# Storing layer 1's rows in rank order and gathering them by rank at the turn to layer 3, in a four-layer graph network

## The chip, the cores and the metric

The kernel runs on one core of one Trainium2 chip. The metric is the device time of one launch in microseconds (us), the median over runs. The core has TensorE (PE; its weight loads are listed apart as PEld), VectorE (DVE), ScalarE (ACT), GpSimd (POOL) and SyncE (SP). Each engine works through its own instructions in order; they wait for each other by semaphores. DMAs are issued here from SyncE, from ScalarE and, where rows are picked by an index (gather and scatter), from GpSimd; an instruction that waits holds up everything behind it in its engine's queue, DMAs included.

## The reference

Four layers over 2708 nodes with 128 features and an adjacency matrix of 2708 x 2708, of which about 0.6% is not zero. Each layer adds its result to its input and normalises over the features:

```python
x = _layernorm(x + _L0_gnn_ref(x, adj))       # (adj.T @ x) / column sums of adj
x = _layernorm(x + _L1_gnn_ref(x, adj, ...))  # messages: gelu(s_i + d_j + b), summed over j with adj_ij, an update MLP
x = _layernorm(x + _L2_gnn_ref(x, adj, ...))  # batch-normed adj @ (x @ W), leaky relu with 0.2
x = _layernorm(x + _L3_gnn_ref(x, adj, ...))  # GATv2 attention, 4 heads, weighted by adj
```

What matters here: x after layer 1 (in the kernel x2) is needed twice. Layer 2 multiplies it by W and by the adjacency matrix; and layer 2's residual adds it once more, row by row, to the batch-normed result.

## The kernel before

Nodes are tiled by 128 into 22 blocks (`BLOCKS`; the last has 20 nodes). Layer 0 is dense. In layers 1 and 3 the kernel uses lists of each node's neighbours, which it finds from the adjacency rows (`extract`, `lists`, `place`), and it sorts the nodes by how many neighbours they have: `rank[n]` is the place of node n in that order, and `perm` is the reverse, the node that stands at a place. Layer 1 works on blocks in rank order, layer 2's result and the batch norm on blocks in node order.

*Layer 1, the loop over 22 blocks* (`for i, b in enumerate(TURNS)`). `own_row` loads a block's rows `x_s` by SyncE (L868, three buffers). `messages` gathers neighbours' rows, one GpSimd gather of 128 rows for each place in the lists (L249, called at L905 through `gather_spaced`, which puts a clear of 200 bytes, L263, between two gathers of a table) into `msg` (five buffers of up to 8 gathers); VectorE adds (L907), ScalarE applies gelu (L910), VectorE weighs and sums (L893, L895). `spread` (L629 to L648) prepares layer 3's lists beside it. `update` runs TensorE (L921, L930 to L932), ScalarE (`agg_t` L928, gelu L937) and VectorE (L938 to L946), ends in `x_n`, the block's rows of x2 (L332 through `normalised`), sends them away (L947, the line that the change edits) and multiplies them by W of layer 2 (L948 to L953) into `xw`.

*Beside it*: `transposed` brings blocks of the adjacency matrix through TensorE transposes (L980), ScalarE copies (`at_sb`, three buffers, L985) and SyncE stores (L987) to `at_dram`, which holds the transposed matrix. The adjacency rows come by SyncE (L417) into the tiles of `ring`, nine slots of 128 x 2708 floats. From turn 11 on `layer2(k)` gathers rows of `at_dram` by `perm` into the same ring (`at_rows`, L1016) and accumulates in six PSUM banks (L1029; the column sums are put in by L1025).

*The turn to layer 3* (L1107 to L1246). When the banks are complete, VectorE and ScalarE compute the batch norm's mean and scale (L1132 to L1156) in `hb`; `masks(g)` makes seven sets of masks for layer 3 from index patterns that GpSimd writes (`jrow` L1158, `row_of` L1166, `start` L1168). Then, four blocks at a time, hb is scaled (L1196 to L1198), the residual x2 is added (L1201), the rows are normalised, scattered in rank order by GpSimd (`x3_dram`, L1215, through the helper at L266) and multiplied into layer 3's table `t2_dram`. Layer 3's own gathers (`g4`) start when that table is written.

*What sets the order.* Between L848 and L1246 a scheduler orders each engine's instructions by the program's order and its own estimate of when each is ready; in parts of layer 0 and in layer 3 the order is written out by hand. Tiles of a closed pool give up their place in memory to pools that are opened later, and these wait for the last use. The ring is opened as the first pool of layer 1 and closed with it.

The rows of x2 go through memory: the scatter at L947 puts the row at place p of block b into row `perm[p, b]` of `x2_dram`, so the table is in node order, and two loads of SyncE (L1114, L1115) bring it back whole.

Of the kernel before, what the change touches and what calls it, by code (L numbers as in the profile page):

```python
# [9 lines left out]
FP = mybir.dt.float32  # L10
# [5 lines left out]
P = 128  # L16
N = 2708
D = 128
NFULL = N // P
NREM = N - NFULL * P  # L20
NBLK = NFULL + 1
# [38 lines left out]
RING = 9  # L60
LW = 2 * SLOTS + 2
BLOCKS = [(b * P, min(P, N - b * P)) for b in range(NBLK)]
# [23 lines left out]
def gnn_resnorm_kernel(  # L86
# [21 lines left out]
    nc = tc.nc  # L108
# [135 lines left out]
    def natural(dram, b0, b1):  # L244

        return dram[b0 * P : b1 * P, :].rearrange("(b p) w -> p b w", p=P)
# [18 lines left out]
    def scatter(table, index, rows):  # L265
        return nc.gpsimd.indirect_dma_start(  # L266
            out=table,
            out_offset=bass.IndirectOffsetOnAxis(ap=index, axis=0),
            in_=rows,
            in_offset=None,  # L270
        ).ins
# [69 lines left out]

    graph = ExitStack()
    own_ps = graph.enter_context(tc.tile_pool(name="own_ps", bufs=1, space=PSUM))

    def banks(name):
        return [bank.tile([P, 512], FP, name=f"{name}{i}", tag="bank") for i in range(6)]

    with ExitStack() as layer:
        ring = layer.enter_context(tc.tile_pool(name="ring", bufs=RING))
        work = layer.enter_context(tc.tile_pool(name="work", bufs=1))  # L350
        small = layer.enter_context(tc.tile_pool(name="small", bufs=2))
        engine = mybir.EngineType
# [312 lines left out]
        for g in KINDS:  # L665
            j = 32 // g
# [250 lines left out]
        def update(b, x_s, x_st, parts):  # L917
            n = BLOCKS[b][1]
            tp = tail_ps.tile([P, 512], FP, name="tail")
            for i in range(2):  # L920
                nc.tensor.matmul(  # L921
                    tp[:, 0:n], lhsT=parts[0:n, i, :], rhs=ident[0:n, 0:n],
                    start=(i == 0), stop=(i == 1),
                )
            x_b = mine.tile([P, D], FP, name="x_b")
            nc.vector.tensor_tensor(x_b[0:n], x_s[0:n, 1, :], lnb[0:n], ALU.add)
            agg_t = mine.tile([P, P], FP, name="agg_t")
            nc.scalar.copy(agg_t[:, 0:n], tp[:, 0:n])  # L928
            pn = tp[0:n, P : 2 * P]
            nc.tensor.matmul(pn, lhsT=x_st[:, 0:n], rhs=u1_t, start=True, stop=False)  # L930
            nc.tensor.matmul(pn, lhsT=ones[0:1, 0:n], rhs=updb[0:1, :], start=False, stop=False)
            nc.tensor.matmul(pn, lhsT=agg_t[:, 0:n], rhs=u2_t, start=False, stop=True)  # L932
            new = mine.tile([P, 1, D], FP, name="new")
            x_n = mine.tile([P, 1, D], FP, name="x_n")
            sums = mine.tile([P, 2], FP, name="sums1")
            h, s0, s1 = new[0:n, 0, :], sums[0:n, 0:1], sums[0:n, 1:2]
            nc.scalar.activation(h, pn, AF.Gelu)  # L937
            nc.vector.scalar_tensor_tensor(  # L938
                h, h, 1.0, x_s[0:n, 1, :], ALU.mult, ALU.add, accum_out=s0
            )  # L940
            rstd = deviation(mine, n, 1, new[0:n], s0)
            nc.vector.scalar_tensor_tensor(h, h, s0, lnw[0:n], ALU.add, ALU.mult)
            nc.vector.scalar_tensor_tensor(
                h, h, rstd[0:n, 0:1], x_b[0:n], ALU.mult, ALU.add, accum_out=s1
            )
            normalised(mine, n, 1, new[0:n], s1, x_n[0:n])  # L946
            scatter(x2_dram, perm[0:n, b : b + 1], x_n[0:n, 0, :])  # L947
            nc.tensor.transpose(tp[:, 256 : 256 + n], x_n[0:n, 0, :], ident[0:n, 0:n])  # L948
            x_nt = mine.tile([P, P], FP, name="x_nt")
            nc.scalar.copy(x_nt[:, 0:n], tp[:, 256 : 256 + n])  # L950
            px = tp[0:n, 384:512]
            nc.tensor.matmul(px, lhsT=x_nt[:, 0:n], rhs=w2_l2, start=True, stop=True)
            nc.scalar.copy(xw[0:n, b, :], px)  # L953
# [58 lines left out]
        def layer2(k):  # L1012

            b, n = TURNS[k], BLOCKS[TURNS[k]][1]
            at = ring.tile([P, N], FP, name="at_rows", tag="rows")
            gather(at[0:n, :], at_dram, perm[0:n, b : b + 1])  # L1016
            weighed = small.tile([P, P], FP, name="weighed", bufs=1)
            nc.scalar.activation(
                weighed[0:n], ones[0:n], AF.Copy, scale=column_sum[0:n, b : b + 1]
            )  # L1020
            for ib in range(NBLK) if k == 0 else ORDER:
                i0, m = BLOCKS[ib]
                if ib == 21:

                    nc.tensor.matmul(  # L1025
                        accs2[5][:, 2 * D : 3 * D], lhsT=weighed[0:n], rhs=xw[0:n, b, :],
                        start=False, stop=False,
                    )
                nc.tensor.matmul(  # L1029
                    accs2[ib // 4][0:m, (ib % 4) * D : (ib % 4 + 1) * D],  # L1030
                    lhsT=at[0:n, i0 : i0 + m],
                    rhs=xw[0:n, b, :],
                    start=(k == 0 and ib % 4 == 0),
                    stop=(k == NBLK - 1 and ib in (3, 7, 11, 15, 19, 20)),
                )
# [10 lines left out]
        for i, b in enumerate(TURNS):  # L1046
# [34 lines left out]
            if i >= 11:  # L1081
                for k in range(2 * (i - 11), min(i, 2 * (i - 10))):
                    layer2(k)
        layer2(NBLK - 1)

# [21 lines left out]
    with ExitStack() as layer:  # L1109
        work = layer.enter_context(tc.tile_pool(name="bn", bufs=1))  # L1110
        small = layer.enter_context(tc.tile_pool(name="bn_small", bufs=2))
        hb = work.tile([P, NBLK, D], FP, name="hb")
        x2 = work.tile([P, NBLK, D], FP, name="x2")
        nc.sync.dma_start(x2[:, 0:NFULL, :], natural(x2_dram, 0, NFULL))  # L1114
        nc.sync.dma_start(x2[0:NREM, NFULL, :], x2_dram[NFULL * P : N, :])  # L1115
        a_all = keep.tile([P, HEADS, D], FP, name="a_all")
        nc.scalar.dma_start(a_all, att.partition_broadcast(P))
        w1_sb = keep.tile([P, HEADS, D], FP, name="w1_s")
# [75 lines left out]
        for b0, count, n in quads():  # L1194
            h = hb[0:n, b0 : b0 + count]
            nc.vector.tensor_tensor(h, h, broad(scale, n, count), ALU.mult)  # L1196
            nc.vector.tensor_tensor(h, h, broad(beta_row, n, count), ALU.add)
            nc.vector.scalar_tensor_tensor(h, h, 0.2, h, ALU.mult, ALU.max)  # L1198
            sums = small.tile([P, 4], FP, name="sums2")
            for j in range(count):  # L1200
                nc.vector.scalar_tensor_tensor(  # L1201
                    hb[0:n, b0 + j, :], hb[0:n, b0 + j, :], 1.0, x2[0:n, b0 + j, :],
                    ALU.mult, ALU.add, accum_out=sums[0:n, j : j + 1],
                )
            normalised(
                small, n, count, h, sums[0:n, 0:count], xs[0:n, b0 : b0 + count, :],
                newton=False,
            )
            w = (count - 1) * P + n
            nc.sync.dma_start(  # L1210
                t2_dram[b0 * P : b0 * P + w, HD : HD + D].rearrange("(b p) w -> p b w", p=n),
                xs[0:n, b0 : b0 + count, :],
            )
            for b in range(b0, b0 + count):
                did = scatter(x3_dram, rank[0:n, b : b + 1], xs[0:n, b, :])  # L1215
                for before in sent:
                    tc.declare_no_dep(
                        did, before, query=mybir.DependencyQuery.ANY_SYNC,
                        reason="each row has a place of its own",
                    )  # L1220
                sent.append(did)
            pt = bank.tile([P, 512], FP, name="pt_x3", tag="bank")
            for j in range(count):
                nc.tensor.transpose(
                    pt[:, j * P : j * P + n], xs[0:n, b0 + j, :], ident[0:n, 0:n]
                )
            xt = small.tile([P, 512], FP, name="xt3")
            nc.scalar.copy(xt[:, 0:w], pt[:, 0:w])
            for j in range(count):
                at = slice(j * P, j * P + n)  # L1230
                pm = bank.tile([P, 512], FP, name="pm_t", tag="bank")
                nc.tensor.matmul(pm[0:n], lhsT=xt[:, at], rhs=w2_sb, start=True, stop=True)
                pa = bank.tile([P, 512], FP, name="pa_t", tag="bank")
                nc.tensor.matmul(
                    pa[0:n, 0:HEADS], lhsT=xt[:, at], rhs=w_a2, start=True, stop=True
                )
                row = small.tile([P, HD], FP, name="t_row", bufs=4)
                nc.scalar.copy(row[0:n], pm[0:n])
                beta_t = small.tile([P, HEADS], FP, name="beta_t", bufs=4)
                nc.vector.tensor_copy(beta_t[0:n], pa[0:n, 0:HEADS])  # L1240
                r0 = (b0 + j) * P
                nc.sync.dma_start(t2_dram[r0 : r0 + n, 0:HD], row[0:n, :])
                nc.sync.dma_start(t2_dram[r0 : r0 + n, HD + D : RW], beta_t[0:n, :])
# [865 lines left out]
```

## Time and profile before

| what | value |
|---|---|
| median of three runs (lowest to highest) | 1891.95 us (1882.17 to 1901.53) |
| the profiled execution, time and span | 1903.62 and 1901.9 us |
| mean granted TensorE clock | 0.719 |
| busy: PE, PEld, DVE, ACT, POOL | 1279.9, 876.6, 1118.4, 822.5, 1094.0 us |
| GpSimd gathers in layer 1 / layer 2 / layer 3 | 368 / 22 / 400 |
| last x_n of layer 1 ends | 1011.1 us |
| layer 2's banks complete | 1020.8 us |
| first row block added at L1201 | 1043.5 us |
| first gather of layer 3's table | 1100.6 us |

All times that follow from the profile belong to one profiled execution, which took 11.7 us more than the median of the runs. A row of the groups reads: line, engine, operation, what it writes <- what it reads, how often, then busy time in us and mean ns of one, then the engine's idle time before it and what ended that. Digits in names are left out, so `x_dram` stands for `x2_dram` and `x3_dram`; what is read tells them apart. A matmul of 32-bit floats leaves two records. The starts of TensorE's records tell when an instruction was taken up, their ends are modelled; that TensorE was late shows in those who wait for it. "remote" as the end of a wait is a semaphore's change that the profile can't put to a recorded instruction.

### The profile page before, as it was taken

How to read it: one execution, taken by the hardware profiler on the slowest of the kernel's cores; microseconds unless marked ns; L12 is line 12 of the kernel's file. 1: busy time of each engine (PE TensorE's matmuls, PEld its weight loads, DVE VectorE, ACT ScalarE, POOL GpSimd, SP SyncE). 2: the span in 40 equal slices, each digit the busy share in tenths (PEclk: the TensorE clock that was granted, in tenths of full speed). 3: DMA queues.
4: the chain of work that ended last, by engine and by line, in shares of the span. 5: the costliest groups of instructions: out<-in, count | busy, mean ns of one | idle time of the engine just before them, and what ended most of it. 6: DMA issues, size and time to landing. Idle time of an engine off the chain costs nothing. (4 is left out here: it accounts for less than half of the span.)

```text
span 1901.9 us, 24866 instructions
## 1 busy us (share of the span) xinstructions
PE 1279.9 (67%) x5971; PEld 876.6 (46%) x5971; DVE 1118.4 (59%) x4643; ACT 822.5 (43%) x3508; POOL 1094.0 (58%) x1771
## 2 busy tenths in 40 slices
PE   7973413453456536556674758998889899788884
PEld 6973302342345435545563324454445455444543
DVE  8997546675534452333446526666667668565663
ACT  3565436443323211111111525565566567455662
POOL 1004777646766375764640476875776777766640
PEclk9986555555555666667766866788788989778785
DMA  8632557566545523324231574865565665745540
GB/s 286 245 138 87 135 130 208 170 172 180 142 119 143 173 66 117 113 95 143 83 104 45 165 226 136 221 199 162 166 201 172 184 185 167 220 139 174 162 115 7
DMA packets 167684, 289.71 MB, mean 152 GB/s; under 512 B 49600, under 2 KB 121502, under 8 KB 160429
## 3 DMA queue, kind: packets, MB, share of 16 engines
q0 software_dynamic: 60496, 190.77, 34.2%
q1 hardware_dynamic: 99489, 92.57, 15.7%
q10 hardware_dynamic: 7544, 4.69, 1.0%
q8 instruction: 50, 0.82, 0.2%
q14 instruction: 105, 0.86, 0.1%
HBM read 242.51 MB, written 45.36 MB: 151 GB/s over the span
## 5 line engine op out<-in xcount | busy, mean ns | idle before, releaser
L249 POOL DMA_INDIRECT g<-t_dram,idx x400 | 403.5, 1009 | 196.2 <-issue 124.8
L249 POOL DMA_INDIRECT msg<-d_dram,idx x368 | 350.3, 952 | 153.9 <-issue 114.5
L1401 ACT ACTIVATE sum_junk<-g 126x128 bf16<-126x128 f32 (+3 forms) x1200 | 352.6, 296 | 39.2 <-ACT sum_junk L1401 21.6
L1375 PE MATMUL z<-g,ident 126*126 126x512 f32 (+3 forms) x400 | 250.0, 757 | 0.6 <-issue 0.6
L1369 PE MATMUL z<-x,copies 32*126 32x512 f32 (+3 forms) x800 | 213.0, 769 | 39.5 <-issue 23.1
L1401 ACT ACTIVATION_READ_ACCUMULATOR sum_junk<-g 126x1 f32 (+3 forms) x1200 | 225.6, 188 | 0.0
L980 PE MATMUL pt_a<-ident,rows 128*128 128x128 f32 (+2 forms) x475 | 118.1, 409 | 136.8 <-issue 68.9
L263 POOL MEMSET pause<- 1x200 int8 x768 | 195.7, 255 | 1.5 <-remote 1.3
L1029 PE MATMUL acc<-x_nat,at_rows 128*128 128x128 f32 (+2 forms) x968 | 169.1, 337 | 32.7 <-issue 21.9
L1029 PEld LDWEIGHTS acc<-x_nat,at_rows 128*128 128x128 f32 (+2 forms) x968 | 152.5, 243 | 49.9 <-issue 35.8
L980 PEld LDWEIGHTS pt_a<-ident,rows 128*128 128x128 f32 (+2 forms) x475 | 86.8, 212 | 159.6 <-issue 78.9
L1375 PEld LDWEIGHTS z<-g,ident 126*126 126x126 f32 (+3 forms) x400 | 83.0, 231 | 166.4 <-issue 155.0
L1447 PE MATMUL po_s<-wm,g 126*128 126x24 f32 (+6 forms) x800 | 117.9, 301 | 53.8 <-DVE wm L1434 38.2
L431 PE MATMUL acc<-x_nat,rows 128*128 128x129 f32 (+3 forms) x1012 | 128.6, 288 | 26.6 <-DMA rows<-in_adj_dram 16.0
L1447 PEld LDWEIGHTS po_s<-wm,g 126*128 126x128 f32 (+3 forms) x800 | 115.1, 227 | 66.2 <-DVE wm L1434 42.1
L895 DVE SCALAR_TENSOR_TENSOR own<-msg,ls,own 128x128 f32<-128x128 f32 (+1 forms) x302 | 106.0, 351 | 66.6 <-ACT msg L910 23.9
L1567 DVE TENSOR_TENSOR g<-g,z 126x1024 f32<-126x1024 f32 (+3 forms) x100 | 121.6, 1216 | 39.4 <-PE z L1369 16.9
L431 PEld LDWEIGHTS acc<-x_nat,rows 128*128 128x128 f32 (+2 forms) x1012 | 122.8, 197 | 32.0 <-DMA rows<-in_adj_dram 17.0
L1393 DVE SCALAR_TENSOR_TENSOR g<-g,a_ps 126x1024 f32<-126x1024 f32 (+3 forms) x100 | 121.1, 1211 | 0.0
L1369 PEld LDWEIGHTS z<-x,copies 32*126 32x126 f32 (+3 forms) x800 | 63.9, 211 | 90.4 <-issue 56.4
L1385 DVE SCALAR_TENSOR_TENSOR g<-z,a 126x128 f32<-126x128 f32 (+3 forms) x400 | 91.6, 285 | 20.4 <-PE z L1375 9.4
L1568 DVE SCALAR_TENSOR_TENSOR g<-z,a 126x512 f32<-126x512 f32 (+3 forms) x100 | 68.6, 686 | 58.8 <-remote 23.2
(302 smaller groups left out, 2164.4 us busy)
## 6 DMA issues: line engine op xcount, KB each, us to landing
rows<-in_adj_dram SPq DMA_DIRECT2D x34, 1354.0 KB
at_dram<-at_sb SPq DMA_DIRECT2D x105, 256.0 KB
g<-t_dram,idx POOLq DMA_INDIRECT x400
msg<-d_dram,idx POOLq DMA_INDIRECT x368
t_dram<-t_row SPq DMA_DIRECT2D x21, 256.0 KB
x_s<-dx_dram SPq DMA_DIRECT2D x21, 128.0 KB
at_dram<-at_sb SPq DMA_DIRECT2D x21, 64.0 KB
t_dram<-x_nat SPq DMA_DIRECT2D x5, 256.0 KB
```

Source lines behind the costliest of these rows:

```text
L249: return nc.gpsimd.indirect_dma_start(out=dst, out_offset=None, in_=table[0:N, :], in_offset=bass.IndirectOffsetOnAxis(ap=index, axis=0),)
L263: paused[table.name] = nc.gpsimd.memset(pause, 0).ins
L431: nc.tensor.matmul(accs0[k][0:m, c0 : c0 + f1 - f0], lhsT=rows[0:n, j0 : j0 + m], rhs=x_nat[0:n, b, f0:f1], start=k not in started, stop=( ...
L895: nc.vector.scalar_tensor_tensor(to, m, v, last, ALU.mult, ALU.add)
L980: nc.tensor.transpose(pt[0:m, j, 0:n], rows[0:n, c0 : c0 + m], ident[0:n, 0:n])
L1029: nc.tensor.matmul(accs2[ib // 4][0:m, (ib % 4) * D : (ib % 4 + 1) * D], lhsT=at[0:n, i0 : i0 + m], rhs=xw[0:n, b, :], start=(k == 0 and i ...
L1369: nc.tensor.matmul(z2[0:e, r, :] if r < 2 else zs[r - 2][0:e], lhsT=copies[g][rows, j, :], rhs=own[b][1][rows, :], start=True, stop=r < 2, ...
L1375: nc.tensor.matmul(zs[r - 2][0:e], lhsT=ident[0:e, 0:e], rhs=g4[0:e, r, 0:HD], start=False, stop=True, skip_group_check=True,)
L1393: nc.vector.scalar_tensor_tensor(z, z, 0.0, a_ps[0:e].unsqueeze(1).to_broadcast((e, 2, HD)), ALU.max, ALU.mult)
L1401: nc.scalar.activation(junk[0:e], g4[0:e, r, hd * D : (hd + 1) * D], AF.Identity, accum_out=sc[0:e, r, hd : hd + 1],)
L1447: nc.tensor.matmul(po[:, p0 * HEADS : (p0 + g) * HEADS], lhsT=g4s[i][0:e, r, HD : HD + D], rhs=wm[0:e, 4 * i + r, :, :], start=True, stop= ...
L1567: nc.vector.tensor_tensor(z, z, z2[0:e], ALU.add)
```

## The change

Three things. The row blocks of layer 1 are stored as they are, in rank order, by a plain store that SyncE issues, in place of GpSimd's scatter. After the last `layer2` 22 gathers of GpSimd, one a block, fetch x2 by `rank`, so that each block arrives in node order; they go into two tiles that take slots of the ring (21 blocks in the one, the last block in the other), and L1201 reads them there. The two loads and the tile x2 of the batch-norm pool go. For this the ring is opened outside of layer 1, on the other side of the memory, and is kept until the batch norm is done. The gathers of layers 1 and 3 keep the clears between them, as before.

```diff
     own_ps = graph.enter_context(tc.tile_pool(name="own_ps", bufs=1, space=PSUM))
+    ring = graph.enter_context(tc.tile_pool(name="ring", bufs=RING, side="right"))
...
     with ExitStack() as layer:
-        ring = layer.enter_context(tc.tile_pool(name="ring", bufs=RING))
...
             normalised(mine, n, 1, new[0:n], s1, x_n[0:n])
-            scatter(x2_dram, perm[0:n, b : b + 1], x_n[0:n, 0, :])
+            nc.sync.dma_start(x2_dram[b * P : b * P + n, :], x_n[0:n, 0, :])
...
         layer2(NBLK - 1)
+        x2_full = ring.tile([P, N], FP, name="x2_full", tag="rows")
+        x2_last = ring.tile([P, N], FP, name="x2_last", tag="rows")
+        x2 = [x2_full[:, b * P : b * P + D] for b in range(NFULL)] + [x2_last[:, 0:D]]
+        for b in range(NBLK):
+            n = BLOCKS[b][1]
+            gather(x2[b][0:n, :], x2_dram, rank[0:n, b : b + 1])
...
-        x2 = work.tile([P, NBLK, D], FP, name="x2")
-        nc.sync.dma_start(x2[:, 0:NFULL, :], natural(x2_dram, 0, NFULL))
-        nc.sync.dma_start(x2[0:NREM, NFULL, :], x2_dram[NFULL * P : N, :])
...
-                    hb[0:n, b0 + j, :], hb[0:n, b0 + j, :], 1.0, x2[0:n, b0 + j, :],
+                    hb[0:n, b0 + j, :], hb[0:n, b0 + j, :], 1.0, x2[b0 + j][0:n, :],
```

## The prediction

> **What bounds the kernel now.** I read the core's clock and span (one core, 0.719 granted), the busy shares and the slices, the GpSimd groups, the waits of 640 to 1021 us, the timeline there and at 1010 to 1060 us, and the SyncE timeline. The whole-span shares (PE 67%, DVE 59%, POOL 58%) name no bound; the stretches that the change touches do. Layer 1's block loop runs from 300 to 1011 us; the gathers of layer 2 (at_rows) join it at 636 us. GpSimd's groups first:
>
> ```profile
> L249 POOL DMA_INDIRECT msg<-d_dram,idx x368 | 350.3, 952 | 153.9 <-issue 114.5 <-ACT at_sb L985 31.3 <-DMA x_s<-dx_dram 4.5
> L266 POOL DMA_INDIRECT x_dram<-x_nat,rank x22 | 22.0, 998 | 18.6 <-DVE x_nat L332 12.3 <-issue 4.1 <-DMA t_dram<-beta_t 1.4
> L266 POOL DMA_INDIRECT x_dram<-x_n,perm x22 | 21.9, 996 | 135.6 <-DVE x_n L332 96.1 <-DVE own L895 31.6 <-DVE own L893 5.1
> ```
>
> The third line is what the change removes (digits are dropped, so x_dram is x2_dram here and x3_dram above): 21.9 us of work and 135.6 us in which GpSimd stood in front of it, with message gathers queued behind. That looks like a large prize. The waits of 640 to 1021 us say otherwise (engine, line, releaser: us, times, longest):
>
> ```profile
> ACT agg_t L928 <- remote: 99.7, 6, 25.1
> POOL x_dram L266 <- DVE x_n L332: 96.1, 8, 17.0
> ...
> DVE msg L907 <- DMA msg<-d_dram,idx: 4.6, 1, 4.6
> ```
>
> The messages' consumer (L907) waited 4.6 us for a gather in all: the gathers are early. What holds a block is the first line, ScalarE's copy of agg_t, which waits for TensorE's L921. TensorE is slow just then; the table by stretch shows when (us, then PE, PEld, DVE, ACT, POOL busy and count, PE clock, DMA share, GB/s):
>
> ```profile
> 670.00:682.00 12.00, 5.30 (x16) 3.62 (x16) 1.04 (x6) 0.00 (x0) 10.35 (x17) 0.60 0.17 49
> 682.00:688.00 6.00, 5.07 (x31) 5.06 (x31) 3.19 (x16) 1.41 (x4) 0.00 (x0) 0.67 0.04 11
> 805.00:817.00 12.00, 2.27 (x11) 1.98 (x10) 0.77 (x4) 0.00 (x0) 10.54 (x19) 0.50 0.15 44
> 817.00:829.00 12.00, 9.77 (x51) 8.69 (x51) 4.84 (x29) 2.38 (x9) 0.72 (x1) 0.63 0.42 137
> 1013.00:1021.00 8.00, 7.66 (x48) 7.24 (x48) 0.22 (x2) 0.15 (x1) 0.18 (x2) 0.74 0.02 7
> ```
>
> While GpSimd issues gathers and VectorE and ScalarE are nearly idle, TensorE passes 16 records in 12 us (0.75 us each) and 11 in 12 us; with GpSimd idle, 31 in 6 us (0.19), 51 in 12 us (0.24) and 48 in 8 us (0.17). A block's delay ends when GpSimd's run of gathers ends:
>
> ```profile
> 816.77 0.95 POOL L249 DMA_INDIRECT at_rows<-at_dram,perm  x1 [0.16 <-issue]
> ...
> 819.72 0.27 ACT L928 COPY agg_t<-tail 128x128 f32<-128x128 f32 x1 [17.73 <-remote]
> ```
>
> The same at 413.7 and 415.0, 855.8 and 854.4, 889.5 and 893.8 us. So from 640 us on a block is: 13 us of messages, a wait to the end of GpSimd's run, some 12 us of update, and only then the scatter and the next run. What slows TensorE I can't read off. [...]
>
> **The change, part by part.** I sum against the profiled execution (span 1901.9, time 1903.62); the three runs have the median 1891.95, 11.7 lower, and the differences are added to that.
>
> (A) *22 scatters leave GpSimd.* Each took 0.996 us and 0.30 before the next issue, 1.3 together. Where GpSimd's run ends a block's delay, the run is 1.3 us shorter. Between the end of L921 in the record and L928 lie 2.1, 6.8, 13.4, 9.3, 13.8, 4.7 and 11.0 us in the seven blocks from 743 to 954 us, 61 in all; 7 x 1.3 = 9 us gained. The 135.6 us of waiting don't come on top, I think: msg has five buffers, a block of 16 to 18 gathers needs three, so the next gathers wait for buffers that the message phase frees, and that phase starts where the scatter was released (x_n at 831.2, messages from 831.1). Best end: GpSimd uses the two free buffers during the update, ends its runs earlier, and all 61 us go. Worst end: gathers now run beside the update, whose 18 or so TensorE records go from 0.2 to 0.75 us: 10 us in 9 blocks, 90, less the 61: +29. I take -9, since the buffers decide.
>
> (B) *22 stores enter SyncE's queue*, each waiting for x_n. Issue is 0.3 us each (x_s<-dx_dram 0.33), hidden: from 640 us on SyncE does little but wait for an x_s buffer (L868 <- DVE new L938, 223.9 us in 9). From 300 to 640 us the stores of at_dram, the adjacency loads and the list loads queue behind. x_n comes 8 us after L938 (782.7 to 790.8). Seven at_dram stores go out in 12.18 us at 382.75, 1.74 each, so three at_sb buffers cover 5.2 us; 2.8 us exposed in each of 11 blocks is +31, the upper end. If SyncE comes to the store after x_n, 0. ScalarE waited for these stores only 19.8 us in all, so I stay near the low end: +3.
>
> (C) *22 gathers at the turn to layer 3.* All of x2_dram is read, so the first waits for the last store: x_n ends at 1011.1, 0.3 to issue, 1.6 to land (lists_dram's scatter, issued till 459.9, released the next at 461.5): 1013.0. Unspaced they cost 0.97 + 0.30 as the x3 scatters do: 22 x 1.27 = 28 us, to 1041, the last landing at about 1043. First need:
>
> ```profile
> 1020.84 0.80 SPq L1114 DMA_DIRECT2D x<-x_dram  x1
> 1043.53 0.28 DVE L1201 SCALAR_TENSOR_TENSOR hb<-hb,x 128x128 f32<-128x128 f32 x1
> ```
>
> The two loads that go were hidden, and worth nothing. L1201 reads the 22 blocks from 1043.5 to 1074.7, so the batch-norm statistics hide the new gathers too. Two other things aren't hidden. First, these gathers stand beside the last 48 TensorE records (1013.2 to 1020.8), with VectorE idle for 9.67 us: just the state of 670 to 682. At 0.75 us 37 records pass till 1041, the other 11 at 0.17 by 1042.9: 22 us late. Second, the iotas of the masks (jrow, row_of, start; 1020.8 to 1021.5 now) come after the gathers in the program; if they run at 1041, 12 us of mask work of VectorE leaves its place ahead of L1196. Then scale is ready at 1032.8 (L1154 ends at 1031.5, reciprocal 0.94, L1156 0.28) and L1196 starts there, not at 1039.1: 6 us gained, up to 8 with the reciprocal's delay. Ends: -8 (TensorE not slowed, masks out of the way) and +22 (slowed, masks first). I take 22 - 8 = +14, by the row whose state is nearest. The x3 scatters queue behind the gathers and started at 1049.75: 9 us of cover; without it each us counts.
>
> The Trainium skill speaks against this part: SBUF — State Buffer, Who interferes with whom, says that VectorE's two-port copies and tensor_scalars lock GpSimd out while it writes descriptors, and gives 3.1 instead of 0.62 us for one such transfer. The row first: x3 scatters issued with VectorE busy took 998 ns against 952 for message gathers, 0.05 more, 1 us over 22. By the page's 3.1 the gathers would end near 1081 and the turn would be some 35 us late; I go by the row. The same section says that TensorE waits for no one at SBUF; no run here has yet shown what else slows it.
>
> (D) *The ring outlives layer 1 and moves to the other side.* Batch-norm and mask tiles fall on layer 1's work tiles, not on the ring; jrow waited 8.45 us for L1029. At best VectorE fills 9.67 us of idle time with masks; with the iotas behind the gathers that is void. 0.
>
> Sum: -9 + 3 + 14 + 0 = +8, so 1891.95 + 8 = 1900.
>
> **The rivals.** (1) *Slower at the turn*: VectorE's fixed order keeps the masks ahead of L1196. Then TensorE ends 22 us late and 12 us of masks wait for iotas at 1041, plus the x3 scatters whose cover is gone (9): 22 + 12 + 9 = +43, less 9: 1926. For it: GpSimd is in order and the gathers precede the iotas; against: TensorE showed no delay at 976 us with GpSimd running. It decides once the gathers end after 1043.5. (2) *SyncE holds at_dram stores*: -9 + 31 + 14 = +36, 1928; for it the 14.04 us of stores at 463.8 around x_n of 473.3; against, 19.8 us of waiting in all. (3) *Faster by look-ahead*: A at -61 with B and C as taken: 1848, half of it 1878; for it, run's end and delay's end coincide; against, five buffers. (4) *It doesn't do what it says*: the 22 gathers use gather, not gather_spaced, so no clear stands between them; the spacing words change no instruction. If they were spaced, each would cost 1.36 us, 2 us in all; that moves nothing.
>
> **How the numbers follow.** Faster or slower by over 1% (19 us) is what a measurement can tell; the three runs alone lie 1% apart. Forecast 0.34, and 0.06 that C comes to -8 (1878): within 1%, 0.40. Rival 1 0.20, rival 2 0.10, A's worst end 0.06: slower 0.36. Rival 3 0.24. The range 1862 to 1938 leaves out the best half of rival 3 and the tail of rivals 1 and 2 with A's worst end, 0.2 together; the likeliest case's own range is 1878 to 1911.
>
> **What would show it.** Right: GpSimd has no x_n group and no wait on L332 before 1011; L928's wait shrinks by some 1.3 us a block; 22 x2 gathers of about 1.27 us from 1013; L1029's last records spread over 20 us beside them; L1196 earlier against the end of L1029. Wrong: L907 begins to wait for gathers, or L985 for stores (B), L928's wait vanishes (A too small), or the last L1029 still takes 8 us (C too large).

## The result, and the profile after

The changed kernel takes 1898.56 us (median of 20 runs, 1884.66 to 1916.47), the kernel before 1889.41 us (20 runs beside it, 1873.31 to 1904.9). The ratio is 1.0055 with a 95% interval of 1.0029 to 1.0080: about 10 us slower, within 1%. Here and below, ratios and intervals are formed from the runs within 1.5% of their kernel's fastest, medians from all runs. The profiled execution of the changed kernel took 1884.66 us (span 1882.9), 13.9 us less than its median, and that of the kernel before 14.2 us more than its own. The two profiles differ by 19 us the other way from the medians; they show where the work stands, not what the change is worth. Stages are therefore compared over several profiles further down.

GpSimd's groups on the page of the changed kernel, and its DMA issues (columns as before):

```profile
L249 POOL DMA_INDIRECT msg<-d_dram,idx x368 | 350.0, 951 | 210.9 <-issue 149.2
...
x_dram<-x_n SPq DMA_DIRECT2D x21, 64.0 KB
```

The group of scatters that read x_n is gone; the stores are SyncE's. But GpSimd's idle time before the message gathers grew from 153.9 to 210.9 us: 57 of the 135.6 us in front of the scatters came back as waits for a free msg buffer. Of the 20 pauses of over 2 us before such a gather, 17 (137 us; before 10 of 13, 80 us) stand before the first gather into a msg tile, which starts 0.7 to 0.9 us after VectorE's last read (L893, L895) of the tile five before it. Another 54.5 us stand at the end, where GpSimd has no gather left and the next index pattern waits for VectorE. The waits of 640 to 985 us in the changed kernel (engine, line, releaser: us, times, longest):

```profile
POOL msg L249 <- issue: 70.0, 129, 13.4
ACT agg_t L928 <- remote: 39.8, 3, 15.5
POOL x_full L249 <- PE tail L952: 12.9, 1, 12.9
```

The wait of L928 that is put down to "remote", 99.7 us in six blocks before, is down to 39.8 in three. GpSimd waits on buffers (70.0 us, before 27.4), and for no x_n until the x2 gathers (12.9 us, put down to TensorE's L952).

The turn, in the timeline of the kernel before and then of the changed one (start and duration in us, engine, line, operation, count, idle before and what ended it). Line numbers behind the edit are 3 higher than before: ps_v is now L1146, `scale` L1156, hb times scale L1199, jrow L1161.

```profile
1020.78 0.29 DVE L1132 SCALAR_TENSOR_TENSOR bn_mean<-acc,b_row 128x128 f32<-128x128 f32 x1 [9.67 <-PE acc L1029]
...
1022.98 6.73 PE L1143 MATMUL ps_v<-bn_sq,ones 128*128 128x128 f32 x42 [2.12 <-ACT bn_sq L1141]
...
1024.32 0.63 ACT L1141 ACTIVATE bn_sq<-hb 128x512 f32<-128x512 f32 x1 [0.79 <-PE ps_v L1143]
...
1030.46 0.29 DVE L1153 TENSOR_SCALAR bn_scale<-ps_v 128x128 f32<-128x128 f32 x1 [2.49 <-PE ps_v L1143]
```

```profile
975.83 0.97 POOL L249 DMA_INDIRECT x_full<-x_dram,rank  x1 [12.91 <-PE tail L952]
...
1003.15 0.91 POOL L249 DMA_INDIRECT x_last<-x_dram,rank  x1 [0.30 <-issue]
1004.09 0.16 POOL L1161 IOTA jrow<- 128x8 int32 x1
...
975.53 7.12 PE L1029 MATMUL acc<-x_nat,at_rows 128*128 128x128 f32 x40 [0.35 <-ACT x_nat L953]
...
991.34 3.42 PE L1146 MATMUL ps_v<-bn_sq,ones 128*128 128x128 f32 x16 [7.60 <-issue]
1003.48 2.08 PE L1146 MATMUL ps_v<-bn_sq,ones 128*128 128x128 f32 x8 [8.72 <-ACT bn_sq L1144]
...
1002.79 0.63 ACT L1144 ACTIVATE bn_sq<-hb 128x512 f32<-128x512 f32 x1 [10.97 <-remote]
...
987.93 0.29 DVE L1135 SCALAR_TENSOR_TENSOR bn_mean<-acc,b_row 128x128 f32<-128x128 f32 x1 [14.50 <-remote]
...
1004.28 0.23 DVE L1173 TENSOR_SCALAR first<-jrow,in 128x8 f32<-128x8 int32 x1 [8.42 <-issue]
...
1012.46 0.29 DVE L1156 TENSOR_SCALAR bn_scale<-ps_v 128x128 f32<-128x128 f32 x1 [7.56 <-PE ps_v L1146]
```

The 22 gathers run from 975.83 to 1004.06 us, 1.25 us each. Beside them TensorE is slow, and those who wait for it show it. bn_mean comes 14.5 us after x_n (before 9.7). ScalarE has two bn_sq buffers and gets the first back, for its third bn_sq, when the eight records that read it are done. They were taken up from 991.34 on, and it gets the buffer at 1002.79, after 11.4 us; before it was 1.3 us (1022.98 to 1024.32). The sum of squares (ps_v) takes 21 us where it took 7.5. The profile doesn't tell whether each record takes long or its end is only passed on late, since the ends are modelled; "slow" stands for both here. VectorE stands 8.42 us for jrow, which waits behind the gathers, and then 7.56 us more for ps_v. From the last x_n (973.4) to the start of the first layer-3 row at L332 pass 57.5 us, before 38.0.

### The profile page after: what moved, and what is told of

Read it like the earlier page. It is cut to its first block, busy times and chain, and to the rows that moved or that the text cites. A ratio compares the mean times of both kernels' runs of the same rounds, so it can differ in the third digit from the quotient of the medians.

```text
span 1882.9 us, 24923 instructions
## 1 busy us (share of the span) xinstructions
PE 1270.4 (67%) x5971; PEld 867.2 (46%) x5971; DVE 1117.0 (59%) x4643; ACT 822.0 (44%) x3508; POOL 1093.2 (58%) x1771
## 5 line engine op out<-in xcount | busy, mean ns | idle before, releaser
L249 POOL DMA_INDIRECT msg<-d_dram,idx x368 | 350.0, 951 | 210.9 <-issue 149.2
L1372 PE MATMUL z<-x,copies 32*126 32x512 f32 (+3 forms) x800 | 202.8, 761 | 35.7 <-issue 13.6
L1029 PE MATMUL acc<-x_nat,at_rows 128*128 128x128 f32 (+2 forms) x968 | 162.4, 331 | 23.3 <-issue 18.9
L1029 PEld LDWEIGHTS acc<-x_nat,at_rows 128*128 128x128 f32 (+2 forms) x968 | 147.1, 237 | 34.4 <-issue 31.5
L1570 DVE TENSOR_TENSOR g<-g,z 126x1024 f32<-126x1024 f32 (+3 forms) x100 | 121.6, 1216 | 46.1 <-remote 19.2
L895 DVE SCALAR_TENSOR_TENSOR own<-msg,ls,own 128x128 f32<-128x128 f32 (+1 forms) x302 | 105.9, 351 | 57.3 <-ACT msg L910 14.5
L910 ACT ACTIVATE msg<-msg 128x896 f32<-128x896 f32 (+4 forms) x55 | 50.4, 917 | 118.2 <-DVE msg L907 68.7
L456 DVE FIND_INDEX8 ci<-cv,rows 128x8 uint32<-128x247 f32 (+2 forms) x242 | 98.8, 408 | 0.0
```

The costliest lines, as they stand in the source:

```text
L249: return nc.gpsimd.indirect_dma_start(out=dst, out_offset=None, in_=table[0:N, :], in_offset=bass.IndirectOffsetOnAxis(ap=index, axis=0),)
L895: nc.vector.scalar_tensor_tensor(to, m, v, last, ALU.mult, ALU.add)
L1029: nc.tensor.matmul(accs2[ib // 4][0:m, (ib % 4) * D : (ib % 4 + 1) * D], lhsT=at[0:n, i0 : i0 + m], rhs=xw[0:n, b, :], start=(k == 0 and i ...
L1372: nc.tensor.matmul(z2[0:e, r, :] if r < 2 else zs[r - 2][0:e], lhsT=copies[g][rows, j, :], rhs=own[b][1][rows, :], start=True, stop=r < 2, ...
L1570: nc.vector.tensor_tensor(z, z, z2[0:e], ALU.add)
```

## The experiments

Twelve runs, in three groups on three chips. On the chips of the first and the third the kernel before takes 1885 and 1892 us, close to the 1889 of the first result; on that of the second it takes 1611, and each run is set against the kernel before on its own chip.

**The parts alone.** The store alone is the kernel before with one line changed:

```diff
-            scatter(x2_dram, perm[0:n, b : b + 1], x_n[0:n, 0, :])
+            nc.sync.dma_start(x2_dram[b * P : b * P + n, :], x_n[0:n, 0, :])
```

> The kernel before with one line changed: the block's rows go out by SyncE's plain store (parts A and B alone). The two loads of x2 stay as they were, so the residual of layer 2 takes rows in rank order: the order of the rows is left out. The prediction's A and B sum to -9 + 3 = -6 us; a result of -3 to -12 bears them out. Rival: if the two profiles are taken at their word (layer 1 37.7 us shorter in the changed kernel, the turn 19.5 us longer), the store gains some 25 to 38 us and the turn gives it back. Second rival: the 37.7 us are the spread of executions and the store gains nothing, 0 within 3 us; then the turn costs only the 9 us seen. Last x_n to first layer-3 normalised row: 38 us as before by all three.

Measured: 1863.34 us, ratio 0.9901 (0.9861 to 0.9940), 18.7 us faster. A and B together are three times what the prediction gave them; the result lies between the -3 to -12 us that would have borne it out and the 25 to 38 of the rival. The waits of 640 to 985 us and the sum of squares:

```profile
POOL msg L249 <- issue: 87.6, 135, 15.0
...
ACT agg_t L928 <- remote: 43.3, 3, 28.2
```

```profile
998.33 5.24 PE L1143 MATMUL ps_v<-bn_sq,ones 128*128 128x128 f32 x42 [2.12 <-ACT bn_sq L1141]
```

L928 waits as in the changed kernel, and with no gathers at the turn ps_v takes its 5 to 6 us. The turn alone is the changed kernel with the scatter put back:

> The changed kernel with the scatter by perm put back (parts C and D alone). The table is then in node order and the 22 gathers by rank fetch rows in another order: the order of the rows is left out. The prediction's C is +14 us (ends -8 and +22). The profiles' turn says +19.5 to +21: last x_n to the first normalised row 57.9 us in place of 38.4. If the gathers alone make the turn late, this kernel is 14 to 21 us slower than before; if it comes out within 5 us, the turn's loss needs the new order of layer 1.

Measured: 1904.07 us, ratio 1.0102 (1.0070 to 1.0133), 19.2 us slower, with the sum of squares as slow as in the changed kernel:

```profile
1017.59 3.79 PE L1146 MATMUL ps_v<-bn_sq,ones 128*128 128x128 f32 x16 [5.37 <-issue]
1028.31 2.07 PE L1146 MATMUL ps_v<-bn_sq,ones 128*128 128x128 f32 x8 [6.94 <-ACT bn_sq L1144]
1036.77 3.83 PE L1146 MATMUL ps_v<-bn_sq,ones 128*128 128x128 f32 x18 [6.38 <-ACT bn_sq L1144]
```

The ring alone:

> The kernel before with nothing but the ring of adjacency rows opened outside of layer 1 and on the other side (part D). The prediction's D is 0: within 3 us of before. Rival: batch-norm and mask tiles then start earlier or later than before, and the turn moves by more than 5 us either way.

Measured: 1887.35 us, 1.0019 (0.9989 to 1.0048): D can't be told from 0 (-2 to +9 us). So the change is two effects of some 19 us with opposite signs.

**Is it jrow's place in GpSimd's queue?** VectorE's 8.42 us for jrow look like rival 1.

```diff
+        jrow = keep.tile([P, 8], I32, name="jrow")
+        nc.gpsimd.iota(jrow, pattern=[[1, 8]], base=0, channel_multiplier=0)
         x2_full = ring.tile([P, N], FP, name="x2_full", tag="rows")
...
-        jrow = ready.tile([P, 8], I32, name="jrow")
-        nc.gpsimd.iota(jrow, pattern=[[1, 8]], base=0, channel_multiplier=0)
```

> The changed kernel with jrow (8 integers a partition) in a place of its own and its index pattern issued ahead of the 22 gathers. In the changed kernel VectorE stood 8.42 us for jrow behind the gathers, and L1199 began at 1019.91, 7.45 us after the batch norm's sum was complete (L1156 at 1012.46). If the queue of index patterns behind the gathers is what costs (rival 1 of the prediction), the masks of the first kind run in the idle time, L1199 starts some 5 us earlier, and the time falls by 5 to 8 us against the changed kernel. If TensorE's slow records set the turn (term C), the sum of squares still ends 39 us after the last x_n and the time falls by 0 to 5 us.

Measured: 1879.08 us, 0.9972 (0.9936 to 1.0008). That is lower than the first measurement of the changed kernel by more than jrow can explain, because the profile says that `scale` came as late as in the changed kernel:

```profile
997.16 0.29 DVE L1137 SCALAR_TENSOR_TENSOR bn_mean<-acc,b_row 128x128 f32<-128x128 f32 x1 [14.41 <-remote]
...
1021.74 0.29 DVE L1158 TENSOR_SCALAR bn_scale<-ps_v 128x128 f32<-128x128 f32 x1 [16.11 <-PE ps_v L1148]
```

The wait for jrow is gone and the wait for ps_v has doubled, from 7.56 to 16.11 us: `scale` is read 39.0 us after the last x_n, as in the changed kernel. To settle it, the patterns of the first three masks too were written ahead of the gathers, beside the changed kernel on one chip:

> The changed kernel with jrow and the patterns row_of and start of the first three masks written into a third slot of the ring, ahead of the 22 gathers, so that no mask waits behind them. Where the kernel before takes some 1611 us, TensorE kept its pace beside the gathers (44 records of ps_v in 5.9 us) and VectorE's 13.40 us for jrow were what the turn lost: there this gains some 8 to 13 us on the changed kernel, about 0.98 of before. Where the kernel before takes some 1885 us, TensorE's 44 records of ps_v took 21 us beside the gathers and end after them: there it is worth what jrow ahead was worth (0.9972 of before), within 5 us. Rival: the order that VectorE gets is as bad with the patterns early, and nothing is gained on either.

> The changed kernel a third time. If the sign depends on how slow TensorE's records are beside GpSimd's gathers, it is 0.983 to 0.990 of before where the kernel before takes some 1611 us, and 1.000 to 1.008 where it takes some 1885 us. If the two comparisons differed for another reason (the chip's other speeds), a ratio between the two may come out on either.

Measured: patterns ahead 1896.59 us, 0.9983 (0.9942 to 1.0024); the changed kernel 1889.17 us, 1.0000 (0.9966 to 1.0033). Nothing is gained: on these chips TensorE, not the queue of patterns, sets the turn. The two intervals of the changed kernel overlap only from 1.0029 to 1.0033; taken together it is 0 to 10 us slower.

**What slows TensorE?** GpSimd being busy, or its gathers? The gathers were replaced by clears of a ring slot, x2 came by two loads of SyncE:

```diff
-            gather(x2[b][0:n, :], x2_dram, rank[0:n, b : b + 1])
...
+        did = nc.gpsimd.tensor_copy(held, xw[0:1, TURNS[-1], 0:1])
+        with tc.issue_after(did.ins):
+            for b in range(NBLK):
+                nc.gpsimd.memset(busy[:, 0:1344], 0.0)
```

> The changed kernel without the 22 gathers: two loads of SyncE bring x2 in rank order (the order of the rows is left out), and GpSimd clears a slot of the ring 22 times (1344 columns, some 1.3 us each) in the gathers' place. It asks what slows TensorE at the turn where the kernel before takes some 1885 us. If it is that GpSimd is busy, bn_scale comes 35 to 39 us after the last x_n, as with the gathers (39.1 and 39.6); if it is the gathers' own descriptors and transfers, it comes 18 to 21 us after, as with the store alone (18.5). Where the kernel before takes some 1611 us TensorE isn't slowed by the gathers either, and 18 to 21 us tell nothing.

Measured on a chip where the kernel before takes 1892 us (one run, 1867.51 us); a stretch (columns as in the prediction's table) and the timeline:

```profile
983.00:994.00 11.00, 9.61 (x51) 8.64 (x51) 0.61 (x5) 0.53 (x2) 2.70 (x4) 0.65 0.47 134
```

```profile
994.24 8.86 POOL L1097 MEMSET busy<- 128x1344 f32 x7
...
996.33 6.58 PE L1153 MATMUL ps_v<-bn_sq,ones 128*128 128x128 f32 x42 [2.59 <-ACT bn_sq L1151]
...
997.57 0.63 ACT L1151 ACTIVATE bn_sq<-hb 128x512 f32<-128x512 f32 x1 [0.78 <-PE ps_v L1153]
...
1003.66 0.29 DVE L1163 TENSOR_SCALAR bn_scale<-ps_v 128x128 f32<-128x128 f32 x1 [1.75 <-PE ps_v L1153]
```

GpSimd clears without a pause from 994 to 1003 us and TensorE keeps its pace: the third bn_sq starts 1.24 us after the first record of ps_v, and `scale` is read 20.4 us after the last x_n. It is the gathers that slow TensorE, not a busy GpSimd. Nor is it the amount of data alone: from 983 to 994 us, with SyncE's loads of x2 under way, 134 GB/s move beside the last records of L1029, and bn_mean comes 10.4 us after x_n; in the changed kernel 58 GB/s move there (973 to 988 us), and it comes after 14.5.

**The second chip.** Four kernels ran where the kernel before takes 1611.11 us. The changed kernel once more:

> The changed kernel once more, beside the others on one chip. The parts alone gave -18.7 us (store) and +19.2 us (turn), which sum to 0; the kernel as a whole was measured at 1.0055 of before, +10 us. If the parts add, it comes out at 0 to +5 us; if they interact, at +10 again, and its profile shows a layer 1 that is longer than with the store alone or a turn that is longer than with the gathers alone.

Measured: 1587.44 us, 0.9863 (0.9838 to 0.9888): the same program is 1.4% faster than before here, 22 us, which neither expected value allowed for. Its timeline at the turn:

```profile
840.77 5.24 PE L1146 MATMUL ps_v<-bn_sq,ones 128*128 128x128 f32 x42 [2.12 <-ACT bn_sq L1144]
...
857.57 0.91 POOL L249 DMA_INDIRECT x_last<-x_dram,rank  x1 [0.30 <-issue]
858.50 0.16 POOL L1161 IOTA jrow<- 128x8 int32 x1
...
858.70 0.23 DVE L1173 TENSOR_SCALAR first<-jrow,in 128x8 f32<-128x8 int32 x1 [13.40 <-POOL jrow L1161]
```

On this chip TensorE isn't slowed: 42 records in 5.24 us with the gathers beside them, ScalarE's third bn_sq 1.24 us after the first of them, and ps_v is done at 846.7. Here rival 1 reads as what the turn loses: VectorE waits 13.40 us for jrow. Patterns ahead should gain there; that kernel ran on another chip, so this stays untried.

Holding the gathers back until `scale` is read:

```diff
-        for b in range(NBLK):
-            n = BLOCKS[b][1]
-            gather(x2[b][0:n, :], x2_dram, rank[0:n, b : b + 1])
...
+        held = keep.tile([1, 1], FP, name="held")
+        done = nc.gpsimd.tensor_copy(held, scale[0:1, 0:1])
+        with tc.issue_after(done.ins):
+            for b in range(NBLK):
+                n = BLOCKS[b][1]
+                gather(x2[b][0:n, :], x2_dram, rank[0:n, b : b + 1])
```

> The changed kernel with the 22 gathers of x2 moved behind the first three masks and held by GpSimd until the batch norm's variance is read (a copy of one element of bn_scale goes before them). If the gathers slow TensorE (16 records of ps_v took from 991.34 to 1002.72 us beside them, 0.71 us each), bn_scale comes about 20 us after the last x_n, as in the kernel before (19.4) and with the store alone (18.5), and not 39 us; VectorE then waits for the gathers at L1204, but four blocks need only 4 x 1.25 = 5 us. Total: 12 to 20 us below the changed kernel, 5 to 10 below before. If TensorE is slow at the turn for another reason, bn_scale stays at some 39 us and the time rises by the 28 us of gathers that are no longer hidden.

Measured: 1595.57 us, 0.9908 (0.9887 to 0.9929), 8 us more than the changed kernel there, where 12 to 20 less were expected. `scale` is read 18.7 us after the last x_n, as expected, but on this chip ps_v ends as early beside the gathers (18.5 us), so the run says nothing on TensorE. (The 0.71 us each of the expectation count 16 records; the buffer that came back is read by eight, so it is an estimated 1.4 us, if all of the 11.4 us is theirs.) The gathers then stand before the x3 scatters:

```profile
879.55 0.90 POOL L249 DMA_INDIRECT x_last<-x_dram,rank  x1 [0.31 <-issue]
881.32 1.03 POOL L266 DMA_INDIRECT x_dram<-x_nat,rank  x1
```

The first scatter starts 15 us after the first row is ready (866.5), and the turn is 97.4 us long where the changed kernel's is 89.8.

Two kernels divided A into the wait and the issue:

```diff
-            scatter(x2_dram, perm[0:n, b : b + 1], x_n[0:n, 0, :])
+            to_send.append((b, x_n))
...
+                    scatter(x2_dram, perm[0:n, b : b + 1], x_n[0:n, 0, :])
...
             x_st, agg = messages(b, x_s, three)
+            send(1)
```

> The kernel before with each scatter of x2 issued one block later, behind the next run of message gathers (three x_n buffers), so that GpSimd no longer stands before it. All 22 scatters remain, and so do the two loads at the turn. If A is the wait for x_n, which kept the next run of gathers from starting, this gains most of what the store alone gained: 10 to 19 us below before. If A is the 1.3 us that each scatter lengthens a run by (the prediction's reading), it gains nothing: within 5 us of before.

Measured: 1604.16 us, 0.9962 (0.9945 to 0.9978), 6 us faster. And the wait without the scatter:

```diff
-            scatter(x2_dram, perm[0:n, b : b + 1], x_n[0:n, 0, :])
+            nc.sync.dma_start(x2_dram[b * P : b * P + n, :], x_n[0:n, 0, :])
+            nc.gpsimd.tensor_copy(pause_f, x_n[0:1, 0, 0:1])
```

> The kernel before with SyncE's store in place of the scatter, and with GpSimd made to wait for each x_n all the same: it copies one element of x_n where the scatter stood. The order of the rows of the residual is left out. If A is the wait, this comes out at before, within 5 us; if A is the time of the issue (0.996 + 0.30 us each), it gains as the store alone did, 10 to 19 us, less the copies.

Measured: 1601.92 us, 0.9942 (0.9919 to 0.9964), 9 us faster. Neither gains the 10 to 19 us that were expected of the half that matters, nor nothing. GpSimd's groups from 600 us to the last x_n, the changed kernel (to 830 us), the scatter later and the wait alone (both to 852 us):

```profile
L249 POOL DMA_INDIRECT msg<-d_dram,idx x127 | 120.5, 949 | 23.4 <-issue 21.5 <-DVE own L895 0.5 <-ACT x_st L882 0.3
```

```profile
L266 POOL DMA_INDIRECT x_dram<-x_n,perm x10 | 10.1, 1008 | 10.8 <-DVE own L894 9.2 <-issue 0.7 <-DVE idx L643 0.2
```

```profile
L949 POOL COPY pause_f<-x_n 1x1 f32<-1x1 f32 x11 | 1.9, 177 | 40.0 <-DVE x_n L333 40.0
```

On this chip GpSimd issues with no pause of over 1.3 us from 600 us to its last message gather at 793 us in the changed kernel, so each issue and each wait there counts. With the scatters later it stands 9.2 us before them and issues ten; with the wait alone it stands 40.0 us. Both end layer 1 some 24 us later (852 us, the changed kernel 828). The halves alone bring 6 and 9 us. Both together are worth some 30 us in layer 1: the 22 us that the changed kernel gains, and 8 that its turn gives back (89.8 us against 81.8 and 81.3).

The kernel before once more, for a second profile:

> The kernel before once more, for its profile on this chip. Where it takes some 1885 us: the delays from the last L921 to L928 sum to 90 to 105 us over the 22 blocks. Where it takes some 1611 us: they sum to under 20 us, as in the other kernels there, layer 1 from the first message gather to the last x_n takes some 650 us and the turn some 82 us; then GpSimd's issues (1.3 us for each of 22 scatters, 29 us) set the pace of layer 1 from 600 us on, and not TensorE.

It took 1884.78 us (one run); the delays from the start of the last L921 to L928 sum to 95.4 us, as expected for a chip of this pace.

**Stages over the profiles of the first result and of the first and third groups** (us, ends of VectorE's x_n at L332, and the first gather of layer 3's table). Four kernels have the scatter (before twice, ring alone, turn alone), six the store:

| | 10th x_n | 16th | 19th | 22nd (last) |
|---|---|---|---|---|
| scatter, mean of four | 626.9 | 824.4 | 924.5 | 1001.9 |
| store, mean of six | 611.0 | 819.6 | 925.2 | 981.7 |
| difference | -16 | -5 | +1 | -20 |

| last x_n to first gather of layer 3 | us |
|---|---|
| no x2 gathers (before twice, ring alone, store alone, clears) | 89.5, 92.9, 92.6, 92.2, 93.8 |
| x2 gathers (changed twice, turn alone, jrow ahead, patterns ahead) | 108.9, 109.6, 106.9, 106.0, 108.6 |

The means are 92.2 and 108.0: the turn costs 15.8 us. Layer 3, which neither touches, is 783 to 802 us long whichever kernel it is; that is the spread behind single profiles.

## Why the prediction was right, and where its steps were not

The time (+10 us measured, +8 forecast) was right in part by luck. The parts measured -18.7 and +19.2 us where the prediction had -6 (A and B) and +14 (C and D): errors of 13 and 5 us on terms of opposite sign, which cancel in part. The parts sum to 0, and the change itself came out at +10 and at 0 in two comparisons on such chips; +8 lies between.

*(A), -9 us: A and B together measured -18.7, and the step that failed is "7 x 1.3".* It takes a block's delay to end with GpSimd's run, so that it shrinks by the scatter's own 1.3 us. In the profile before, that holds for 6 of the 13 delays of over 2 us between L921 and L928, and for 4 of the 7 that the prediction summed; after the others the next gather follows within 1.3 us, in the midst of a run. In the changed kernel all 8 such delays end in the midst of a run. What the scatter's leaving brought is look-ahead: gathers that ran in these delays run elsewhere. The delays, from the start of the last L921 to L928, sum over the 22 blocks to 91 to 103 us with the scatter (four profiles) and to 57 to 83 with the store (six).

The table shows where the time is. 16 us are gained by the 10th block, a part for which the prediction had no term. From there to the 19th block all of it is lost again, which is the "worst end" of (A), gathers beside the update: in blocks 11 to 19, 75 to 93 gathers are issued between L928 and x_n, with the scatter 36 to 43, and these stretches sum to 167 to 181 us, with the scatter 139 to 143. And 20 us come in the last three blocks. There the gathers are out. The last message gather in the timeline, of the changed kernel (69 us before the last x_n) and then of the kernel before (26 us):

```profile
904.24 0.95 POOL L249 DMA_INDIRECT msg<-d_dram,idx  x1 [0.16 <-issue]
```

```profile
985.00 0.95 POOL L249 DMA_INDIRECT msg<-d_dram,idx  x1 [0.16 <-issue]
```

Look-ahead was doubted because of five msg buffers; GpSimd ran ahead all the same. That the prediction took the buffers as decisive was half right: 57 of the 135.6 us in front of the scatters came back as buffer waits.

*(B), +3 us.* SyncE does stand in front of the stores, but nobody waits much for it: ScalarE waited for at_dram stores 19.8 and 28.2 us in two profiles of before, 33.0, 24.0 and 33.1 us in the changed kernel (twice) and with the store alone. B isn't measured apart from A; rival 2 (+31) is out, since the sum is -18.7 and these waits grew by at most some 13 us.

*(C), +14 us, held in kind: +19.2 with the turn alone, 15.8 in the profiles.* The mechanism is the one named, slow records of TensorE beside the gathers, but its place was missed, and with it the split. The prediction put +22 on the last 48 records of L1029; they cost some 4 (bn_mean comes 13.2 to 15.3 us after x_n with gathers, 9.7 to 10.5 without). The sum of squares behind them, which it took as unslowed, costs 15: from bn_mean to `scale` it is 24.2 to 26.5 us with gathers, 8.2 to 10.0 without. And the -8 for masks that leave their place is -1: L1199 comes 7.5 us after `scale` where it came 8.6. The first gather started 2.4 us after x_n at 1.25 us each (predicted 1.9 and 1.27).

*(D), 0:* 1.0019, with an interval that holds 1.

*The rivals.* (1) is half true: VectorE's fixed order keeps masks ahead, and the wait for jrow shows, but on these chips ps_v ends last and the wait is free; on the second chip it reads as what the turn costs. (3), look-ahead, is what A turned out to be, without going to -61 on these chips. (4): the x2 gathers stand 0.30 us apart with no clear between them, as read from the code; spacing them wasn't tried.

The forecast doesn't hold on the second chip. The -22 us there are rival 3's (-44 us, half of it -14): A is worth some 30 us (22 and the turn's 8), and C is only the wait for jrow.

No kernel here is shown to be better than both kernels on every chip. With jrow ahead, the interval still reaches 1; the scatter later was tried on the second chip alone; the store alone is faster, but it leaves out the order of the rows.

## What to carry to other kernels

An instruction that goes from an in-order queue can be worth more than its own time and its wait taken singly: on the second chip the halves brought 6 and 9 us, both together some 30. When it moves to a place that looks idle, price what it does to the engine that works there, all the way to the next hand-over: the 28 us of gathers were hidden behind the batch norm, and on the slower chips they cost 16 to 19 us by slowing the matmuls of that batch norm. Before a one-per-cent change is kept or dropped, run it on another chip.

## What the runs showed of the hardware

TensorE's results come late beside GpSimd's indirect gathers on some chips and not on another. The same program took 1889 to 1899 us and 1587 us. Up to the first message gather the profiles are equal (202.3 and 202.0 us from the start of the span); then layer 1 takes 768 against 626 us and layer 3 792 against 671. Twelve microseconds of layer 1 in the changed kernel, on the third chip and then on the second (PE, PEld, DVE, ACT, POOL busy and count, PE clock, DMA share, GB/s):

```profile
700.00:712.00 12.00, 3.55 (x21) 2.91 (x20) 0.00 (x0) 0.27 (x1) 10.13 (x18) 0.71 0.67 261
```

```profile
700.00:712.00 12.00, 9.28 (x62) 8.57 (x63) 7.47 (x27) 2.40 (x5) 10.67 (x18) 0.75 0.59 228
```

Beside 18 instructions of GpSimd each, TensorE passes 21 records on the one chip, with VectorE and ScalarE idle behind it, and 62 on the other, at granted clocks of 0.71 and 0.75: the clock doesn't tell them apart. It isn't the same block in the two, so the records show the state and not a rate. Without gathers the slower chips are as fast as the other: 42 records of ps_v in 5.24 us in both (store alone, and the second chip). The same work compared, from the first record of ps_v to ScalarE's third bn_sq, takes 9.3 to 12.6 us beside the gathers in the five profiles on the slower chips, and 1.2 to 1.3 without them and on the second chip. The Trainium skill, SBUF — State Buffer, Who interferes with whom, says that PE never waits on anyone. On the slower chips those who wait for TensorE get its results late beside indirect gathers all the same; that it waits at SBUF isn't shown, and the run with clears says that it isn't GpSimd's own writing to SBUF. Which part of a gather it is, its descriptors or its transfers, and what differs between the chips, stays open.
